# Two decoder-like layers on one core: twelve probability buffers for the second layer's attention, comparisons on another engine, a new order of stages

## The chip, the core and the metric

The kernel runs on one core of a Trainium2 chip. A core has a matrix engine (TensorE, in the profile PE, with its weight loads as PEld), three engines for elementwise work (VectorE as DVE, ScalarE as ACT, GpSimd as POOL) and a sync engine (SP) that here issues nearly all transfers. Each engine takes its instructions in one fixed order; semaphores make one engine wait for another. The metric is the device time in microseconds (us) of one execution. Three executions of the kernel before took 678.07, 679.97 and 681.12 us, median 679.97 us.

## What is computed

The input is a batch of 4 sequences of 512 tokens with 256 channels, in f32. Two layers follow, each a "macaron": half a feed-forward block, attention, half a feed-forward block, with a layer norm ahead of each.

```python
x = x + 0.5 * L0_ffn(layernorm(x)); x = x + L0_attn(layernorm(x)); x = x + 0.5 * L0_ffn(layernorm(x))
x = x + 0.5 * L1_ffn(layernorm(x)); x = x + L1_attn(layernorm(x)); x = x + 0.5 * L1_ffn(layernorm(x))

# L0_ffn: weights are integers minus 128 with a scale per row; silu(gate) * up, then down; hidden 704
# L0_attn: 16 heads of 16 channels, rotary embedding, causal softmax
# L1_ffn: weights made ternary; sigmoid(x @ w1.T) * (x @ w2.T), then @ w3.T
def _quantize(w):
    gamma = jnp.mean(jnp.abs(w))
    return jnp.clip(jnp.round(w / (gamma + EPS)), -1.0, 1.0)
# L1_attn: 16 query heads, 4 key/value heads, ALiBi slopes as bias, causal softmax, output bias
```

## The kernel before, in words

All activations stay in on-chip memory: `X[b]` holds one sequence as 128 partitions x 4 chunks x 256 channels. There are 24 stages of coarse work, for each sequence `b` and layer `L` a feed-forward, an attention and a feed-forward, and they are mixed with each other.

How the order comes about matters here. Every stage is cut into small closures (one tile of a matmul with its evaluation, one score unit, one load). Each closure gets a due time from the table `PLAN` (line 32), in units of one head group of attention; there are 32 such groups, and a unit is a little under 20 us. The closures are sorted by due time (line 694) and recorded in that order. A scheduler of the framework then sets each engine's final order, from that order, the dependencies and the buffers that are free. So an edit of one number in `PLAN`, or of the engine of one operation, may move instructions on all engines.

**Attention.** Each sequence and layer has four groups `g` of four heads. The queries and keys of a group are stacks `Qs[g]` and `Ks[g]` in bf16, 128 partitions x 4 heads x 512 tokens: three bf16 parts of each number, stacked so that one bf16 matmul gives a product of nearly f32 accuracy. `fills(g)` (line 429 and on) loads the stacks from DRAM, with three transfers of 128 KB for `Qs` and, in layer 0, three for `Ks`, issued by SP. In layer 1 there are only 4 key heads in all, so one stack per sequence is enough: `kst` (line 500) takes `Ks[b % 2]`. `Ks[2]` and `Ks[3]` are not used in layer 1, and the rotary tables `cst` (cosine and sine) are not either.

`pass1(g)` (line 503) computes scores in a PSUM tile of tag "s" (four buffers, shared with pass 2), and VectorE takes the row maximum under the mask (line 517, a custom instruction and a short one that reads the accumulator). `fin` (line 521) transposes the maxima and sends them as two more rows into `Qs[g]`, so that pass 2 subtracts the maximum in the matmul itself. `pass2(g)` (line 538) computes the scores transposed (line 557), ScalarE takes the exponential into a buffer of tag "P" (lines 553 and 562), GpSimd sets the part above the diagonal to zero (line 564), and `pv` (line 568) multiplies with the values, for four heads at once on four groups of 32 columns of the matrix engine. The tag "P" has `NP` = 6 buffers of 128 x 512 f32. An exponential into a used buffer waits until the `pv` matmul that read it is done.

**Feed-forward.** `mtile` (line 306) is four matmuls of 128 x 512 into a PSUM tile, with the activations split into a high and a low part. `act` (line 319) is the activation: ScalarE and VectorE read the tile, and GpSimd or VectorE make the low part (line 353). `down` (line 359) is the second projection.

**Layer 1's ternary weights.** `load_ffn1` (line 165) reads the 11 pieces of the three weight matrices twice. The first round (`sums`) takes the sum of absolute values on ScalarE (line 173), 12 instructions with an accumulator; `level` (line 176) makes the thresholds `thr`; the second round (`quant`, line 187) loads each piece again into one of the four buffers of tag "tmp" and makes `(w > t) - (w < -t)` in two instructions: the `is_lt` comparison on GpSimd (line 190), then `is_gt` with the subtraction on VectorE (line 191). Eight pieces have 128 x 352 elements (into `GU[1]`), three 128 x 512 (into `WD[1]`). The feed-forward blocks share the tag "tmp". The rounds are due at `PLAN["w1"]`.

Of the kernel before, what the change touches and what calls it, by code (L numbers as in the profile page):

```python
# [10 lines left out]
F32 = mybir.dt.float32  # L11
# [4 lines left out]
ALU = mybir.AluOpType  # L16
# [4 lines left out]
T = 512  # L21
# [8 lines left out]


PLAN = {
    "lnw": 0.1082, "dw": 0.02, "va": -3.2452, "w1": (3.23, 5.1402, 5.278, 5.8437), "la": 10.0549, "lo": 17.0054,
    "F000": (-4.7797, -3.9955, 0.5991, 0.627), "F010": (-2.4824, -1.3829, 0.446, 0.02),
    "F020": (-1.3638, -1.0988, 0.2537, 0.02), "F030": (0.0651, 4.5821, 0.553, 0.052),
    "F001": (5.6832, 7.2392, 0.5108, 0.5201), "F100": (8.4901, 9.5646, 0.227, -0.008),
    "F011": (10.2798, 11.8688, 0.4612, -0.091), "F110": (12.6033, 13.3522, 0.4119, -0.0508),
    "F021": (13.7131, 15.2214, 0.2194, 0.6814), "F120": (16.1663, 17.4558, 0.1237, 0.057),
    "F031": (17.7427, 19.2089, 0.1794, 0.3572), "F130": (20.6648, 21.4405, 0.097, 0.191),
    "F101": (22.2359, 24.7912, 0.25, 0.0563), "F111": (25.133, 28.5272, 0.2253, 0.559),  # L40
    "F121": (30.9876, 31.9389, 0.3174, 0.35), "F131": (32.8792, 34.4424, 0.45, -0.035),
    "q": (-5.4943, -4.6753, -4.4887, -3.8, -3.9803, -3.4013),
    "q0": (-2.5968, -2.298, -2.236, -1.8988, -1.881, -2.3597),
    "q1": (-0.825, -0.405, -0.485, 0.081, -0.5019, 0.7836), "fill0": -1.2442, "fill": 0.044,
    "p1": (0.0178, 1.0178), "p10": (-1.1381, -0.5831), "p11": (-0.4778, -0.4629), "p2": (-0.0092, 0.9501),
    "post": (4.1583, 4.2211), "f2": 0.0459,
}
# [4 lines left out]
NP, NTMP, NRT, NH, NH5 = 6, 4, 4, 5, 1  # L52
# [4 lines left out]
def macaron(ctx, tc, x, gu0, wd0, s0, sd0, wa0, wq1, wkv1, wo1, bo1, gu1, wd1,  # L57
            cs, krow, qrow, out):
    nc = tc.nc
    V, S, G, PE, SY = nc.vector, nc.scalar, nc.gpsimd, nc.tensor, nc.sync  # L60

    con = ctx.enter_context(tc.tile_pool(name="con", bufs=1))
    wrk = ctx.enter_context(tc.tile_pool(name="wrk", bufs=2))
# [18 lines left out]
    for i in range(2):  # L82
# [12 lines left out]
                    fill=NEG, base=0, channel_multiplier=1)  # L95
# [30 lines left out]
    def load_ffn0():  # L126
# [12 lines left out]
        for k in range(3):  # L139
            w = wrk.tile([128, 2, D], I32, tag="P", name=f"wds{k}", bufs=NP)  # L140
            SY.dma_start(w, wd0[:, 2 * k:2 * k + 2])
# [5 lines left out]
    thr = con.tile([128, 6], F32, name="thr")  # L147
# [17 lines left out]
    def load_ffn1():  # L165

        def sums(n, i, src):
            def f():
                if n == 0:
                    G.memset(ab, 0.0)  # L170
                w = piece(src, f"ws{n}")
                for k, v in enumerate([w] if n < 10 else [w[:, 0], w[0:64, 1]]):
                    S.activation(v, v, AF.Abs, accum_out=ab[0:v.shape[0], n + k:n + k + 1])
            return f

        def level():
            V.tensor_reduce(sm[:, 0:2], ab[:, 0:8].rearrange("p (i n) -> p i n", i=2), AX.X, ALU.add)
            V.tensor_reduce(sm[:, 2:3], ab[:, 8:12], AX.X, ALU.add)
            pg = pmm.tile([128, 512], F32, tag="mm", name="pgam")
            ones = wrk.tile([128, T], F32, tag="tmp", name="ones", bufs=NTMP)[:, 0:128]  # L180
            G.memset(ones, 1.0)
            PE.matmul(pg[:, 0:3], ones, sm[:, 0:3], start=True, stop=True)
            V.tensor_scalar(thr[:, 0:3], pg[:, 0:3], 1.0 / (HID * D), EPS_Q, ALU.mult, ALU.add)
            V.tensor_scalar(thr[:, 3:6], thr[:, 0:3], -0.5, None, ALU.mult)
            V.tensor_scalar(thr[:, 0:3], thr[:, 0:3], 0.5, None, ALU.mult)

        def quant(n, i, src, dst):
            def f():
                w = piece(src, f"wq{n}")
                G.tensor_scalar(dst, w, thr[:, 3 + i:4 + i], None, ALU.is_lt)  # L190
                V.scalar_tensor_tensor(dst, w, thr[:, i:i + 1], dst.bitcast(F32), ALU.is_gt, ALU.subtract)
            return f

        ps = list(ffn1_pieces())
        return ([sums(n, i, s) for n, (i, s, d) in enumerate(ps)] + [level] +
                [quant(n, i, s, d) for n, (i, s, d) in enumerate(ps)])
# [6 lines left out]
    cst = con.tile([128, 2, T], F32, name="cst")  # L203
# [39 lines left out]
    Ks = [con.tile([128, 4, T], BF, name=f"Ks{i}") for i in range(4)]  # L243
# [135 lines left out]
        return th, [act(i) for i in ((0, 1, 2, 5, 3, 4) if first else (5, 0, 1, 2, 3, 4))], [down(0), down(1)]  # L379


    def attn(L, b, tag):
        quick = L == 0 and b == 0
        th, xo = layernorm(b, tag, "xa", 1, halves=quick)
        va = VA[b % 2]
# [114 lines left out]
        def kst(g):  # L500
            return Ks[g] if L == 0 else Ks[b % 2]
# [36 lines left out]
        def pass2(g):  # L538
            Q, K = Qs[g], kst(g)
            nr = mr + 2  # L540
            o = [None]
            def steep(h):

                return L == 1 and g == 0 and h == 0

            pt = {}

            def expo(kc, hs):

                def f():  # L550
                    N = T - 128 * kc
                    n = len(hs)
                    P = wrk.tile([128, T], F32, tag="P", name=f"P{g}{kc}{hs[0]}{tag}", bufs=NP)
                    P = P[:, 0:n * N].rearrange("p (h n) -> p h n", h=n)
                    p = psc.tile([128, T], F32, tag="s", name=f"s2_{g}{kc}{hs[0]}{tag}")
                    for i, h in enumerate(hs):
                        PE.matmul(p[:, i * N:i * N + N], K[0:nr, h, kc * 128:(kc + 1) * 128],  # L557
                                  Q[0:nr, h, kc * 128:T], start=True, stop=not steep(h))
                        if steep(h):
                            PE.matmul(p[:, i * N:i * N + 128], identb, maskT, start=False, stop=True)  # L560
                        pt[kc, h] = P[:, i]
                    pt["last"] = S.activation(P, p[:, 0:n * N].rearrange("p (a n) -> p a n", n=N), AF.Exp, scale=0.25)
                    if not steep(hs[-1]):
                        pt["last"] = G.affine_select(P[:, :, 0:128], P[:, :, 0:128], pattern=[[0, n], [1, 128]],
                                                     compare_op=ALU.is_ge, fill=0.0, base=0, channel_multiplier=-1)
                return f

            def pv(kc):


                def f():
                    if kc == 0:
                        o[0] = pov.tile([128, T], F32, tag="o", name=f"o{g}{tag}")
                    with tc.high_priority(20):
                        for h in range(4):
                            hv = 4 * g + h if L == 0 else h
                            m = PE.matmul(o[0][32 * h:32 * h + 32, kc * 128:T], va[:, kc, hv * VS:hv * VS + 32],  # L577
                                          pt[kc, h], start=kc == 0, stop=kc == 3)
                            if kc < 3 and h < 3:
                                tc.add_manual_dep(m.ins if hasattr(m, "ins") else m, (pt["last"].ins if hasattr(pt["last"], "ins") else pt["last"]).name, AFTER, reason="side by side")  # L580
                return f

            us = []
            for kc in range(NC):
                n = (1, 1, 2, 4)[kc]
                us += [expo(kc, tuple(range(h, h + n))) for h in range(0, 4, n)] + ([pv(kc)] if kc < 2 else [])
            us += [pv(2), pv(3)]

            ot = [None]

            def evac():
                ot[0] = wrk.tile([128, T], F32, tag="oT", name=f"oT{g}{tag}", bufs=1)
                S.copy(ot[0], o[0])

            def fin():
                if g == 0:
                    co["c"] = wrk.tile([128, NC, D], F32, tag="ctx", name=f"ctx{tag}", bufs=1)
                ctxt, oT = co["c"], ot[0]
                pt = pmm.tile([128, NC, 4, 32], F32, tag="mm", name=f"ot{g}{tag}")
                for c in range(NC):  # L600
                    PE.transpose(pt[:, c].rearrange("p i e -> p (i e)"), oT[:, c * 128:(c + 1) * 128], ident)
                ri = wrk.tile([128, NC, 4, 1], F32, tag="ri", name=f"ri{g}{tag}")
                V.reciprocal(ri, pt[:, :, :, 16:17])
                V.tensor_tensor(ctxt[:, :, 64 * g:64 * g + 64].rearrange("p c (i e) -> p c i e", e=16),
                                pt[:, :, :, 0:16], ri.to_broadcast([128, NC, 4, 16]), ALU.mult)

            return us + [evac], fin
# [64 lines left out]
    w1 = load_ffn1()  # L672
# [4 lines left out]
    for n in range(8):  # L677
        a = at[n]
        q = PLAN[f"q{n}"] if f"q{n}" in PLAN else [4 * n + v for v in PLAN["q"]]
# [107 lines left out]
```

## Time and profile before

The profiled execution took 676.93 us; its span, from the first to the last instruction, is 675.2 us, so 1.7 us lie around it. That execution is 3.04 us below the median of the three others.

| Engine | busy us of 675.2 | instructions |
|---|---|---|
| PE (matmul) | 643.1 | 4394 |
| PEld (weight load) | 435.1 | 4394 |
| DVE | 527.5 | 1683 |
| ACT | 450.5 | 872 |
| POOL | 396.5 | 643 |

How to read it: matmuls are pipelined, and the matrix engine's records overlap, so "busy" is not full speed; what helps is the idle time of PE, stage by stage, and what ended it. The other engines' busy time tells where they could not have taken more work. The transfers move 45.46 MB, at a mean of 67 GB/s.

### The profile page before, as it was taken

What the parts mean: (1) busy time and instruction counts of PE and PEld (TensorE: products, weight loads), DVE (VectorE), ACT (ScalarE), POOL (GpSimd) and SP (SyncE); (2) the same over time, 40 slices, a digit from 0 to 9 for tenths busy, and PEclk for the clock granted to TensorE, in tenths of its full rate; (3) what the DMA queues carried; (4) which work ended last, traced back from release to release, by engine and by line L of the source; (5) the groups of instructions that cost most, each with busy time, mean ns of one, the idle gap of its engine ahead of it and who ended that gap; (6) DMA issues with size and microseconds to landing.
All of it is one profiled execution on the core that took longest, in us unless ns stands there. A gap on an engine that the chain in (4) does not pass through costs nothing.

```text
span 675.2 us, 13288 instructions
## 1 busy us (share of the span) xinstructions
PE 643.1 (95%) x4394; PEld 435.1 (64%) x4394; DVE 527.5 (78%) x1683; ACT 450.5 (67%) x872; POOL 396.5 (59%) x643
## 2 busy tenths in 40 slices
PE   7798899998989999999999999999999999999987
PEld 5677566455635776667676757767676675565676
DVE  7788899788799797877868686887879678885354
ACT  3674658785668487685858685785847767648633
POOL 3653958666599765586448755595445544434511
PEclk8998999999999999999999999999999999999999
DMA  8204503244442223112210221001200221100000
GB/s 278 91 0 142 141 1 127 73 129 127 148 138 60 83 73 94 43 34 67 65 29 27 74 60 41 25 24 50 60 26 25 70 83 33 50 3 33 0 33 33
DMA packets 30900, 45.46 MB, mean 67 GB/s; under 512 B 6098, under 2 KB 23754, under 8 KB 30830
## 3 DMA queue, kind: packets, MB, share of 16 engines
q1 hardware_dynamic: 30254, 43.88, 21.4%
q10 hardware_dynamic: 576, 0.72, 0.4%
q8 instruction: 35, 0.57, 0.4%
q14 instruction: 35, 0.29, 0.1%
HBM read 32.00 MB, written 12.32 MB: 66 GB/s over the span
## 4 chain that ended last, share of the span: by engine, by line
PE 72%; DVE 9%; DMA 6%; ACT 5%; POOL 4%; issue 3%; SPq 0%; DVEq 0%; ACTq 0%; POOLq 0%
PE pf L315 18%; PE df L367 10%; PE o0a L577 3%; PE o1a L577 3%; PE o2a L577 3%; PE o3a L577 3%; PE po0a L630 2%; PE po1a L630 2%; PE ltf L293 2%; POOL GU L190 1%; DMA wa0s<-in_wa_dram 1%; DMA ws<-in_gu_dram 1%; PE lta L293 1%; DMA gus<-in_gu_dram 1%; PE pq0a L396 1%
## 5 line engine op out<-in xcount | busy, mean ns | idle before, releaser
L315 PE MATMUL pf<-xhf,GU 128*128 128x512 f32 x352 | 122.7, 436 | 4.7 <-ACT xhf L295 2.2
L353 POOL TENSOR_TENSOR hlf<-hf,hhf 128x512 fp32r<-128x512 f32 x72 | 94.1, 1308 | 45.4 <-ACT hhf L352 45.1
L315 PE MATMUL pf<-xlf,GU 128*128 128x512 f32 x352 | 110.2, 400 | 0.6 <-DVE xlf L296 0.5
L557 PEld LDWEIGHTS <-Ks 98*128 98x128 bf16 (+1 forms) x512 | 44.4, 98 | 57.8 <-issue 45.3
L315 PEld LDWEIGHTS pf<-xhf,GU 128*128 128x128 f32 x352 | 61.4, 192 | 27.2 <-ACT xhf L295 5.5
L315 PEld LDWEIGHTS pf<-xlf,GU 128*128 128x128 f32 x352 | 65.8, 189 | 17.1 <-DVE xlf L296 1.5
L513 PEld LDWEIGHTS <-Qs 96*128 96x128 bf16 (+1 forms) x512 | 43.6, 98 | 45.7 <-issue 33.8
L517 DVE DVE_READ_ACCUMULATOR2_ANT mxt<- 128x1 f32 x512 | 71.2, 139 | 0.2
L352 ACT CAST hhf<-hf 128x512 fp32r<-128x512 f32 x80 | 49.8, 623 | 15.6 <-DVE hf L350 11.2
L350 DVE SCALAR_TENSOR_TENSOR hf<-tf,pf 128x512 f32<-128x512 f32 (+1 forms) x48 | 33.0, 686 | 32.3 <-PE pf L315 15.9
L367 PE MATMUL df<-WD,hhf 128*128 128x256 f32 x320 | 55.5, 291 | 2.6 <-ACT hhf L352 2.6
L367 PE MATMUL df<-WD,hlf 128*128 128x256 f32 x320 | 51.8, 287 | 0.2 <-DVE hlf L353 0.2
L367 PEld LDWEIGHTS df<-WD,hhf 128*128 128x128 f32 x320 | 45.5, 192 | 4.6 <-ACT hhf L352 3.0
L367 PEld LDWEIGHTS df<-WD,hlf 128*128 128x128 f32 x320 | 43.9, 191 | 2.1 <-issue 1.4
L345 POOL TENSOR_TENSOR hf<-tf,hf 128x512 f32<-128x512 f32 x30 | 39.3, 1311 | 9.1 <-ACT hf L344 7.0
L289 ACT ACTIVATE xnf<-X,mrf,rsf 128x256 f32<-128x256 f32 x60 | 31.9, 596 | 14.5 <-POOL mrf L269 9.6
L349 ACT ACTIVATE tf<-pf 128x512 f32<-128x512 f32 (+1 forms) x48 | 28.3, 595 | 19.4 <-PE pf L315 19.2
L295 ACT CAST xhf<-ltf 128x512 fp32r<-128x512 f32 x32 | 18.5, 588 | 20.3 <-PE ltf L293 20.2
L341 ACT ACTIVATE tf<-pf,sgh 128x512 f32<-128x512 f32 (+1 forms) x36 | 25.0, 694 | 6.6 <-PE pf L315 6.1
L372 POOL TENSOR_TENSOR X<-X,dtf 128x512 f32<-128x512 f32 x14 | 18.4, 1316 | 18.1 <-DVE dtf L371 15.9
L342 DVE SCALAR_TENSOR_TENSOR tf<-tf,pf 128x512 f32<-128x512 f32 (+1 forms) x36 | 24.5, 681 | 4.2 <-ACT tf L341 4.1
L261 DVE BATCH_NORM_STATS2 bsf<-X 128x6 f32<-128x256 f32 x64 | 23.5, 413 | 3.6 <-POOL X L372 1.9
(534 smaller groups left out, 2065.1 us busy)
## 6 DMA issues: line engine op xcount, KB each, us to landing
Qs<-drqa SPq DMA_DIRECT2D x96, 128.0 KB
Ks<-drka SPq DMA_DIRECT2D x60, 128.0 KB
out_dram<-X SPq DMA_DIRECT2D x8, 256.0 KB
X<-in_x_dram SPq DMA_DIRECT2D x3, 512.0 KB
drka<-raka SPq DMA_DIRECT2D x4, 384.0 KB
drka<-rcka SPq DMA_DIRECT2D x4, 384.0 KB
drqa<-raqa SPq DMA_DIRECT2D x4, 384.0 KB
drqa<-rcqa SPq DMA_DIRECT2D x4, 384.0 KB
```

The lines of the kernel that those rows point to most:

```text
L289: S.activation(xn[c], X[b][:, c], AF.Identity, bias=mr[:, i:i + 1], scale=rs[:, i:i + 1])
L315: PE.matmul(p, w[:, m:m + 128], xx[:, k], start=n == 0, stop=n == 3)
L345: G.tensor_tensor(h, t, h, ALU.mult)
L349: S.activation(t, g, AF.Tanh, scale=0.5)
L350: V.scalar_tensor_tensor(h, t, 1.0, u, ALU.add, ALU.mult)
L352: S.copy(hh, h)
L353: (V if big and i % 2 or (first or last and big) and i > 2 else G).tensor_tensor(hl, h, hh.bitcast(F32), ALU.subtract)
L367: PE.matmul(p[:, cc], ho[l, i][:, ts], WD[L][:, i], start=n == 0, stop=n == 10)
L513: PE.matmul(p[:, i * st:i * st + N], Q[0:mr, h, c * 128:(c + 1) * 128], K[0:mr, h, 0:N], start=True, stop=True)
L517: V.tensor_tensor_reduce(pi, pi, mask[:, T - N:T], 1.0, FLOOR, ALU.add, ALU.max, mx[:, h, c:c + 1])
L557: PE.matmul(p[:, i * N:i * N + N], K[0:nr, h, kc * 128:(kc + 1) * 128], Q[0:nr, h, kc * 128:T], start=True, stop=not steep(h))
L577: m = PE.matmul(o[0][32 * h:32 * h + 32, kc * 128:T], va[:, kc, hv * VS:hv * VS + 32], pt[kc, h], start=kc == 0, stop=kc == 3)
```

## The change

Three things are changed.

1. In `quant`, the comparison `is_lt` is issued on VectorE instead of GpSimd.
2. In layer 1, every second probability tile takes its room from a rotation of six: two halves of each of `Ks[2]` and `Ks[3]`, seen as f32, and the two halves of `cst`. The others keep the tag "P" with its six buffers.
3. Nine numbers in `PLAN` are changed, among them the beginning of the `sums` round (3.23 to 3.7945) and the due time of the stack loads (`fill`, 0.044 to 0.4489 units after the reference point). The rest shift by up to 0.34 units.

```diff
 PLAN = {
-    ... "w1": (3.23, 5.1402, 5.278, 5.8437) ...
+    ... "w1": (3.7945, 5.1402, 5.278, 5.8437) ...
-    "F020": (-1.3638, -1.0988, 0.2537, 0.02)
+    "F020": (-1.3638, -1.0988, 0.0794, 0.02)
-    "F001": (5.6832, 7.2392, ...)   "F110": (12.6033, 13.3522, ...)   "F130": (20.6648, 21.4405, ...)
+    "F001": (5.6832, 7.3715, ...)   "F110": (12.6033, 13.1578, ...)   "F130": (20.6648, 21.4499, ...)
-    "q": (-5.4943, ...)   "q1": (-0.825, -0.405, -0.485, 0.081, -0.5019, 0.7836)   "fill": 0.044
+    "q": (-5.4589, ...)   "q1": (-0.825, -0.3982, -0.485, 0.081, -0.5019, 1.1219)   "fill": 0.4489
...
         def quant(n, i, src, dst):
             def f():
                 w = piece(src, f"wq{n}")
-                G.tensor_scalar(dst, w, thr[:, 3 + i:4 + i], None, ALU.is_lt)
+                V.tensor_scalar(dst, w, thr[:, 3 + i:4 + i], None, ALU.is_lt)
                 V.scalar_tensor_tensor(dst, w, thr[:, i:i + 1], dst.bitcast(F32), ALU.is_gt, ALU.subtract)
...
+    used = [0]
+
+    def spare():
+
+        used[0] += 1
+        room = [k.rearrange("p h t -> p (h t)").bitcast(F32)[:, T * i:T * i + T] for k in Ks[2:] for i in range(2)]
+        room += [cst[:, i] for i in range(2)]
+        return room[used[0] // 2 % 6] if used[0] % 2 else None
...
-                    P = wrk.tile([128, T], F32, tag="P", name=f"P{g}{kc}{hs[0]}{tag}", bufs=NP)
+                    P = spare() if L == 1 else None
+                    if P is None:
+                        P = wrk.tile([128, T], F32, tag="P", name=f"P{g}{kc}{hs[0]}{tag}", bufs=NP)
```

## The prediction

> **What bounds the kernel now.** First the page: the chain that ended last and the busy shares.
>
> ```profile
> span 675.2 us, 13288 instructions
> PE 643.1 (95%) x4394; PEld 435.1 (64%) x4394; DVE 527.5 (78%) x1683; ACT 450.5 (67%) x872; POOL 396.5 (59%) x643
> PE 72%; DVE 9%; DMA 6%; ACT 5%; POOL 4%; issue 3%; SPq 0%; DVEq 0%; ACTq 0%; POOLq 0%
> ```
>
> PE is the bound, and 32.1 us of the span (675.2 - 643.1) are all that it stands idle. A gain has to come out of these, so I cut them by stage. The columns of the next view are the stretch, its length, busy us (with instructions) of PE, PEld, DVE, ACT and POOL, then clock, DMA share and GB/s.
>
> ```profile
> 134.00:149.00 15.00, 14.78 (x98) 8.28 (x97) 12.59 (x44) 12.16 (x28) 9.51 (x16) 1.00 0.42 126
> 149.00:165.00 16.00, 13.23 (x93) 7.74 (x92) 13.24 (x44) 11.20 (x30) 10.50 (x17) 1.00 0.44 139
> 165.00:179.00 14.00, 14.00 (x120) 11.65 (x113) 9.08 (x31) 6.13 (x13) 7.58 (x13) 1.00 0.49 152
> 179.00:190.00 11.00, 10.46 (x73) 5.80 (x72) 10.80 (x43) 8.98 (x22) 9.14 (x16) 1.00 0.36 100
> 190.00:206.00 16.00, 12.65 (x98) 5.79 (x96) 15.64 (x48) 10.27 (x21) 15.93 (x21) 1.00 0.57 165
> 206.00:222.00 16.00, 15.27 (x90) 9.67 (x91) 13.44 (x47) 13.34 (x25) 15.67 (x23) 1.00 0.19 52
> 343.00:600.00 257.00, 254.82 (x1837) 169.61 (x1836) 203.87 (x698) 180.07 (x347) 144.20 (x249) 1.00 0.14 43
> ```
>
> The reader is to see two things: from 343 to 600, nearly all of layer 1's attention, PE idles 2.2 us of 257; from 179 to 206 it idles 3.9 us of 27, and there both POOL (15.93 of 16 in the second part) and DVE (15.64 of 16) are full. Third, what PE waited for in 179 to 207, and the two lines of the ternary weights with the nearest row for the moved comparison (line 124: one source, one constant, the same shapes):
>
> ```profile
> PE o2a L577 <- POOL P203a L564: 1.2, 1, 1.2
> PE o1a L577 <- POOL P130a L564: 0.8, 1, 0.8
> PE s_021a L513 <- DVE mxt L517: 0.4, 1, 0.4
> ```
>
> ```profile
> L190 POOL TENSOR_SCALAR GU<-wq,thr x8: 1158/1181/1758, 185.1 to 196.8; 128x352 fp32r<-128x352 f32 x8
> L190 POOL TENSOR_SCALAR WD<-wq,thr x3: 1564/1564/1994, 200.3 to 204.4; 128x512 fp32r<-128x512 f32 x3
> L191 DVE SCALAR_TENSOR_TENSOR GU<-wq,thr,GU x8: 570/592/840, 186.7 to 198.6; 128x352 fp32r<-128x352 f32 x8
> L191 DVE SCALAR_TENSOR_TENSOR WD<-wq,thr,WD x3: 743/747/1162, 203.8 to 206.9; 128x512 fp32r<-128x512 f32 x3
> ...
> L124 DVE TENSOR_SCALAR GU<-gus x4: 311/326/340, 5.4 to 9.0; 128x352 fp32r<-128x352 int32 x4
> L124 DVE TENSOR_SCALAR WD<-wds x3: 427/428/555, 11.5 to 13.3; 128x512 fp32r<-128x512 int32 x3
> ```
>
> **Part 1, the comparison leaves POOL.** Line 190 took 10.5 + 5.1 = 15.6 us of POOL in 185 to 206. The triangle selections (line 564) stood between these, and two `pv` groups of PE waited for them: 0.82 at 191.6 and 1.23 at 196.9 in the timeline, together 2.05 us. That is the price of POOL on PE here, and all of it may go. The most that could go is PE's whole idle time of 179 to 206, 3.9 us.
>
> **Part 1, it arrives on DVE.** Eight pieces at the line-124 median of 326 ns and three at 428: 2.61 + 1.28 = 3.9 us. Upper bound: as long as line 191, 8 x 0.592 + 3 x 0.747 = 7.0 us. Lower bound: if POOL's traffic is what stretches line 191 from its shortest (570 and 743) to its means (641 and, from 743, 747 and 1162, 884), then 8 x 0.07 + 3 x 0.14 = 1.0 us comes back and 2.9 remain. I take 3.9, since line 124 is nearest in form. What covers it? DVE's idle time in 179 to 206 is 0.20 + 0.36 = 0.56 us; after 206 it has 16 - 13.44 = 2.56. So at 206 DVE is 3.9 - 0.6 = 3.3 us late. Behind the moved instructions in DVE's queue stand the row maxima of the next groups (line 517): until they have read a score tile, PE can't have one of the four "s" buffers back, and PE's fixed order has score matmuls every microsecond here. In the timeline DVE began row maxima 1.1 to 1.4 us after their matmul (192.6 to 193.7, 197.9 to 199.2): PE runs that much ahead, so of 3.3 us I let the buffers swallow 1.1, and PE is 2.2 us late at 206, the POOL waits gone but swallowed by this. From 206 to 222 DVE can catch up 2.56, but PE only its own idle time there, 0.73: net **+1.5 us**. Bounds: -3.9 (POOL alone paced the stretch) and +6.4 (7.0 - 0.6, nothing recovered).
>
> The Trainium skill speaks on both sides here. *GPSIMD Engine Reference*, section "Performance versus the Vector engine", says that VectorE is about twice as fast for elementwise work; by that the moved pieces would take half of 1181 and 1564 ns, 8 x 0.59 + 3 x 0.78 = 7.1 us, an estimate; line 124 against line 190 shows 3.6 times, and the sum goes by that. *Advanced Engine Details and Errata*, section "VectorE Performance Modes", says that a VectorE instruction in a two-port mode and a GpSimd instruction block each other; by it the moved pieces would hold POOL up for as long as they last, so that POOL would gain 11.7 us (15.6 - 3.9) in place of 15.6. No run here shows that yet; the spread of line 191 (570 to 840) while POOL was full is of that kind.
>
> **Part 1, a new wait in DVE's queue.** The moved instruction also waits for its piece's load. A load can start when line 191 has freed its "tmp" buffer four pieces earlier. In the built program's order, DVE has some 4.8 us of work between that release and the comparison (one comparison 0.33, three of line 191 at 0.52 from start to start, two row maxima of 512 columns at 0.73, two short ones 0.43 and 0.48, one low part 0.60). A load of the same kind took from 154.46 (issue on SP) to 157.16, and the next from 155.57 to 160.15, until ScalarE could use them: 2.7 to 4.6 us, plus 0.5 of issue; and pieces 4 to 6 stand behind stack loads on SP (0.6 us an issue). So pieces 4, 5 and 6 may come 0 to 1 us late each. On POOL such a wait held up the selections alone; on DVE it holds up everything. I take +0.5, bounds 0 and +4 (seven pieces, a little over half a microsecond each).
>
> **Part 2, six more probability buffers.** In layer 1, ScalarE waited ten times for a `pv` matmul ahead of an exponential, 9.7 us in total (line 562 released by o0a, o2a, o3a after 313 us). These waits go. But PE has nothing to gain: of its waits in 343 to 600 one is on a probability tile (POOL P013a, 0.3 us), and PE's order there is the same in both builds but for a handful of instructions. Spread over 257 us, the other 2.2 us of idle time end on DVE. I take **-0.3**; bounds -2.2 (all idle time there) and +0.5 (the new rooms in the key stacks are free only when layer 0's last score matmuls have read them; that order is kept in both builds, two groups apart). No instruction is added.
>
> **Part 3, the order.** Up to 139 us the built orders are equal on every engine, so 20% of the span can't change; the changed part is 139 to 345 us, and PE's work per group moves there by at most 1.9 us from one group to the next. Three of the `sums` instructions (0.50 + 0.19 us) move from 142-145 to 149-155, where ScalarE is full: 3 x 0.6 (their spacing) = 1.8 us late on ScalarE, covered by its wait of 3.16 us for the next weight load at 157.2; if that cover is gone, the context cast (line 618), for which PE waited 1.2 us at 161.6, comes up to 1.8 later. On SP, weight loads 5 to 7 still stand behind GpSimd's query parts (lines 413 and 414), so that wait stays. Stack loads move by a place or two among 311 transfers. `pv` groups that are torn apart on PE, and so run twice (275.1 and 276.7 in the timeline, one more microsecond), are 8 before and 6 after, but by their widths 3.4 us of repeated work in both. I take 0, bounds -2 and +2.
>
> **Sum.** 1.5 + 0.5 - 0.3 + 0 = +1.7 us on a span of 675.2, with the 1.7 around it 678.6 for an execution like the profiled one. The median of the runs is 3.0 above that execution, so 679.97 + 1.7 = **681.7 us**: +0.25%, which counts as no change: 0.5% (3.4 us) is about what a measurement of this kernel can tell from none, since its three runs lie 3 us apart. Range of this case alone 677 to 683.4.
>
> **Rivals.** *POOL was the pace-maker* (faster): both its waits and the PE idle time behind them go, DVE's 3.9 us slide behind 206. For it: PE's longest waits in 179 to 206 are on POOL, one on DVE. Against: DVE had 0.56 us free. 679.97 - 3.9 - 0.7 (idle of 206 to 222) = 675.4. Chance 0.18, with the case in it that the buffers of part 2 count (9.7 us were 670).
>
> *DVE becomes the bound* (slower): the comparisons sit in a full queue and also wait for loads; it decides once a load takes longer than about 4.8 us from release to landing, or the comparison takes over 0.5 us. 3.9 + 4 + 1.8 (context cast) - 2.6 (DVE's idle time after 206) = +7.1, hence 687. Chance 0.32.
>
> *The rooms are not free* (part 2 does not do what it says): exponentials would wait on whole stacks instead of halves. The build shows waits on single tiles, so this has 0.02, within slower.
>
> **Numbers.** Forecast 0.50, faster 0.18, slower 0.32. The range takes in the faster rival's figure and the slower one's: 675 to 687.
>
> **What would show it.** Line 190 as DVE rows of 0.3 to 0.5 us at 185 to 207; POOL under 10 of 16 us in 190 to 206; PE's waits on P130 and P203 gone, with waits on DVE's row maxima in their place, and the group after 206 beginning about 2 us later; the stretch 343 to 600 as long as before within 1 us; the first 139 us alike. I am wrong if PE's idle time in 179 to 222 falls by over 3 us, if comparisons wait for loads by more than 2 us in all, or if layer 1's stretch shortens by more than 2 us.

## The result, and the profile after

The changed kernel took 681.09 us (median of 22 runs, 677.77 to 683.79), the kernel before 679.05 us in 22 runs of the same comparison (676.30 to 682.22). The ratio is 1.0029, with a 95% interval from 1.0016 to 1.0043: 2.0 us slower, inside the half per cent that the prediction called no change, but not nothing. The forecast was 681.7 us.

The page of the changed kernel's profiled execution begins so:

```profile
span 681.1 us, 13261 instructions
PE 647.7 (95%) x4394; PEld 437.4 (64%) x4394; DVE 532.0 (78%) x1694; ACT 450.2 (66%) x872; POOL 382.2 (56%) x632
PE 71%; DVE 11%; DMA 5%; ACT 5%; POOL 4%; issue 3%; SPq 0%; DVEq 0%; ACTq 0%; POOLq 0%
```

Eleven instructions left POOL (14.3 us less) and eleven came to DVE (4.5 us more; 3.3 us against the changed kernel with the comparison back on GpSimd, 528.7 us, so that the rest belongs to the other two parts), and DVE's share of the chain that ended last rose from 9% to 11%. This span is 5.9 us longer than that of before, three times the difference of the medians, so a part of it belongs to the executions and not to the kernels; which part is shown at the end of this section.

By stretch of time (columns as in the prediction: stretch, length, busy us of PE, PEld, DVE, ACT and POOL, then clock, DMA share, GB/s), the changed kernel:

```profile
179.00:190.00 11.00, 10.27 (x80) 5.75 (x79) 8.93 (x38) 7.16 (x19) 5.68 (x14) 1.00 0.48 139
190.00:206.00 16.00, 12.79 (x84) 5.37 (x76) 15.61 (x51) 9.41 (x19) 4.60 (x11) 1.00 0.45 129
206.00:222.00 16.00, 14.66 (x80) 8.29 (x78) 14.26 (x43) 10.55 (x20) 8.45 (x13) 0.89 0.23 66
222.00:247.00 25.00, 25.00 (x179) 17.50 (x178) 21.81 (x66) 14.85 (x28) 20.73 (x27) 1.00 0.20 66
343.00:600.00 257.00, 255.16 (x1829) 170.15 (x1827) 205.73 (x704) 180.23 (x348) 146.46 (x254) 1.00 0.15 45
```

In 190 to 206 us POOL fell from 15.93 to 4.60, and PE gained nothing by it: 12.79 busy against 12.65. DVE was full before (15.64) and is full now (15.61). The windows stand at the same times in both profiles, but the changed kernel is 5 to 6 us late there, so they hold not quite the same work; the stretch that is defined below compares like with like. Behind 222 us PE is full in both, so what is late by then stays late. What PE waited for in 179 to 222 us, changed kernel:

```profile
PE s_110a L522 <- DVE mxt L526: 0.8, 1, 0.8
PE pf L315 <- DVE mts3a L537: 0.6, 1, 0.6
PE s_323a L522 <- DVE mxt L526: 0.5, 1, 0.5
PE s_020a L522 <- ACT P203a L573: 0.5, 1, 0.5
PE s_213a L568 <- ACT P212a L573: 0.5, 1, 0.5
...
PE s_100a L522 <- DVE mxt L526: 0.3, 1, 0.3
...
PE o2a L588 <- POOL P203a L575: 0.2, 1, 0.2
```

Of the two waits on GpSimd's selections (2.05 us together) 0.2 is left. In their place stand waits on DVE, 2.4 us against 0.4 in the kernel before, 1.8 of them on row maxima, and waits on ACT's exponentials and casts, 2.3 us against 1.1. ACT itself waited once, 1.5 us, for line 191 (0.3 us before). Last, the ternary weights, each line by itself (min, median and max in ns, then first and last start):

```profile
L190 DVE TENSOR_SCALAR GU<-wq,thr x8: 381/396/402, 189.3 to 200.0; 128x352 fp32r<-128x352 f32 x8
L190 DVE TENSOR_SCALAR WD<-wq,thr x3: 481/483/628, 206.3 to 210.8; 128x512 fp32r<-128x512 f32 x3
its engine sat idle before it (us, times) until:
  DMA wq<-in_gu_dram: 0.3, 1
```

```profile
L191 DVE SCALAR_TENSOR_TENSOR GU<-wq,thr,GU x8: 566/578/768, 191.4 to 202.5; 128x352 fp32r<-128x352 f32 x8
L191 DVE SCALAR_TENSOR_TENSOR WD<-wq,thr,WD x3: 659/747/1650, 208.9 to 213.3; 128x512 fp32r<-128x512 f32 x3
```

The records of the comparison add up to 8 x 0.396 + 3 x 0.53 = 4.8 us; it waited once for a load, 0.3 us. Records on DVE overlap a little, so that its busy time rises by less (3.3 us, above).

**What belongs to the executions.** The most exact reading of two profiles is the start of one and the same matmul in both: here the first score matmul of an attention group (line 513 or 522). Its lateness against the profile of before, in us, by where it stands there:

| Start in before | 71.6 | 149.1 | 169.3 | 187.8 | 202.3 | 245.5 | 342.0 | 397.1 | 601.5 |
|---|---|---|---|---|---|---|---|---|---|
| changed kernel | +1.82 | +1.82 | +3.51 | +4.86 | +5.77 | +6.89 | +7.99 | +7.18 | +6.47 |
| comparison on VectorE alone | +0.45 | +0.52 | +1.55 | +2.73 | +4.72 | +4.76 | +4.89 | +4.88 | +4.89 |
| rooms alone | +1.27 | +1.27 | +2.99 | +2.99 | +2.97 | +2.35 | +2.35 | +1.73 | +1.01 |

The first column spreads over 3.5 us among the fourteen profiles of this case though the orders are equal there; kernels with the new PLAN lie from -0.37 to +3.13, the others from 0 to +1.83. Then the rooms-alone kernel, whose built order equals that of before over more than half of TensorE's queue, loses 1.72 us between 149 and 169 us. The reason is the granted clock. Changed kernel, and below it the kernel before:

```profile
166.00:168.00 2.00, 2.00 (x13) 0.85 (x12) 2.00 (x6) 2.00 (x5) 1.24 (x3) 0.50 0.01 4
...
210.00:212.00 2.00, 1.68 (x6) 1.09 (x6) 2.00 (x7) 1.58 (x4) 0.29 (x1) 0.56 0.65 195
```

```profile
60.00:62.00 2.00, 2.00 (x11) 2.00 (x11) 1.54 (x3) 1.57 (x3) 0.60 (x1) 0.50 0.17 41
...
166.00:168.00 2.00, 2.00 (x20) 2.00 (x19) 1.81 (x5) 1.02 (x2) 2.00 (x3) 1.00 0.27 72
```

The last four columns are POOL, clock, DMA share and GB/s. Twice here PE has half its clock for 3.4 us, 1.7 us lost each time; behind 40 us the profile of before has such a dip at 59 us only. So the readings below take one stretch, from the fourth group of sequence 1 in layer 0 (169.3 us in before) to the first group of layer 1 (342.0), 172.7 us in before, and subtract what the clock took inside it.

### The profile page after: what moved, and what is told of

Same layout as the page of the kernel before. It is cut to its first block, busy times and chain, and to the rows that moved or that the text cites. A ratio compares the mean times of both kernels' runs of the same rounds, so it can differ in the third digit from the quotient of the medians.

```text
span 681.1 us, 13261 instructions
## 1 busy us (share of the span) xinstructions
PE 647.7 (95%) x4394; PEld 437.4 (64%) x4394; DVE 532.0 (78%) x1694; ACT 450.2 (66%) x872; POOL 382.2 (56%) x632
## 4 chain that ended last, share of the span: by engine, by line
PE 71%; DVE 11%; DMA 5%; ACT 5%; POOL 4%; issue 3%; SPq 0%; DVEq 0%; ACTq 0%; POOLq 0%
PE pf L315 19%; PE df L367 11%; PE o3a L588 3%; PE o1a L588 3%; PE o0a L588 3%; PE o2a L588 2%; PE po1a L641 2%; PE po0a L641 2%; DMA wa0s<-in_wa_dram 1%; PE ltf L293 1%; PE lta L293 1%; PE pq0a L405 1%; PE pq1a L405 1%; DMA gus<-in_gu_dram 1%; DVE mxt L526 1%
## 5 line engine op out<-in xcount | busy, mean ns | idle before, releaser
L367 PEld LDWEIGHTS df<-WD,hlf 128*128 128x128 f32 x320 | 45.3, 197 | 1.2 <-issue 1.0
L575 POOL TENSOR_SCALAR_AFFINE_SELECT Ks<-Ks 128x128 f32<-128x128 f32 (+2 forms) x54 | 18.8, 349 | 34.7 <-ACT Ks L573 34.2
```

Source lines behind the costliest of these rows:

```text
L367: PE.matmul(p[:, cc], ho[l, i][:, ts], WD[L][:, i], start=n == 0, stop=n == 10)
```

## The experiments

The three parts can be had one by one, and all eight combinations were run. "Stretch" is the difference to before of the 172.7 us just named, clock dips subtracted, from one profile each. The experiments ran in three groups, each with its own runs of before, medians 678.03 us (rows 1 to 4), 679.06 (rows 5, 6, 8 and 9) and 678.91 (rows 10 to 13); the changed kernel's row is the comparison above. The ratio is estimated from the single runs and is not the quotient of two medians: for rooms alone that quotient is 0.9980, for GpSimd with the round to 7.7 units 0.9990, both inside their intervals.

| Kernel | median us | ratio to before, 95% interval | stretch us |
|---|---|---|---|
| comparison on VectorE alone | 682.22 | 1.0063 [1.0038, 1.0087] | +3.3 |
| rooms alone | 676.68 | 0.9969 [0.9951, 0.9986] | -0.6 |
| new PLAN alone | 680.09 | 1.0024 [1.0003, 1.0044] | +0.3 |
| changed, comparison back on GpSimd | 678.20 | 0.9994 [0.9974, 1.0014] | -0.1 |
| changed, without the rooms | 681.85 | 1.0039 [1.0025, 1.0054] | +2.7 |
| changed, with the old PLAN | 680.09 | 1.0023 [1.0005, 1.0042] | +3.1 |
| changed | 681.09 | 1.0029 [1.0016, 1.0043] | +2.8 |
| changed, weights' round ends at 7.9 units | 686.87 | 1.0111 [1.0089, 1.0133] | +4.6 |
| changed, each comparison twice | 687.58 | 1.0132 [1.0106, 1.0158] | +6.8 |
| changed, weights' round ends at 7.4 | 680.17 | 1.0016 [1.0000, 1.0032] | +1.6 |
| rooms, GpSimd, round ends at 7.7 | 678.24 | 0.9983 [0.9967, 0.9999] | -0.1 |
| rooms, VectorE, round ends at 7.7 | 683.51 | 1.0062 [1.0043, 1.0081] | +3.6 |
| rooms, three comparisons on VectorE | 677.87 | 0.9983 [0.9968, 0.9998] | +0.6 |

**Each part alone, and part 1 undone.** The first four kernels, in the order of the table. The letters of the theories hold within one group of runs. Comparison on VectorE alone:

```diff
-                G.tensor_scalar(dst, w, thr[:, 3 + i:4 + i], None, ALU.is_lt)
+                V.tensor_scalar(dst, w, thr[:, 3 + i:4 + i], None, ALU.is_lt)
```

> The kernel before with the is_lt comparison on VectorE alone, old table, no extra rooms. Theory A (the forecast: VectorE is full from 179 to 206 us, so the moved work lands on PE): 2.0 us slower (1.5 for the work, 0.5 for waits on loads), ratio 1.003. Theory B (GpSimd paced that stretch): 2 to 4 us faster, ratio 0.995 to 0.997, and the new table costs what the whole change costs. Theory C (the parts are all free, the difference is in the buffers): 1.000.

Rooms alone (the kernel before with `spare()` and its use):

```diff
-                    P = wrk.tile([128, T], F32, tag="P", name=f"P{g}{kc}{hs[0]}{tag}", bufs=NP)
+                    P = spare() if L == 1 else None
+                    if P is None:
+                        P = wrk.tile([128, T], F32, tag="P", name=f"P{g}{kc}{hs[0]}{tag}", bufs=NP)
```

> The kernel before with the six extra probability rooms alone. Theory A: 0.3 us faster, ratio 0.9995 (between 0.997 and 1.001); ScalarE's ten waits on probability products after 313 us (9.7 us) gone, PE's idle time from 343 to 600 us as before within 1 us. Theory B: the same. Theory C: 2 us slower or more, 1.003.

The new PLAN alone (the table's hunk of the change, nothing else):

> The kernel before with the new table alone. Theory A: no change, ratio 1.000 (between 0.997 and 1.003). Theory B: slower by more than the whole change, 1.005 or more, since the comparison's move then gains. Theory C: 1.000.

The changed kernel with the comparison back on GpSimd (the first diff, reversed):

> The changed kernel with the is_lt comparison back on GpSimd; new table and extra rooms stay. Theory A: 2.0 us faster than the changed kernel, so level with the kernel before, 1.000. Theory B: slower than the changed kernel, 1.006 or more of the kernel before. Theory C: as the changed kernel, 1.003.

Measured: +0.63%, -0.31%, +0.24% and, undone, 0.9994. The comparison on VectorE costs time with nothing else changed, and its lateness arises where the prediction put it: in the table of lateness it goes from +1.55 to +4.72 us between 169 and 202 us and is never made good. The rooms are worth much more than was forecast. The result of 2 us is a difference of larger parts.

**The other combinations.** The changed kernel without the rooms, then with the old PLAN:

```diff
-                    P = spare() if L == 1 else None
+                    P = None
```

> The changed kernel without the six rooms (comparison on VectorE and the new PLAN stay). Theory A, the three parts add up, each at its own place: part 1 and the PLAN measured alone gave +0.63% and +0.24%, so 1.0087 of the kernel before; from the changed kernel's side, 1.0029 + 0.0031 = 1.006. So 1.006 to 1.009 (683 to 685 us), and in 380 to 397 us and after 575 us the group marks are 0.5 us each later again than in the changed kernel. Theory B, the rooms pay only in the old order of stages: within 0.001 of the changed kernel, 1.002 to 1.004.

```diff
-    "lnw": 0.1082, "dw": 0.02, "va": -3.2452, "w1": (3.7945, 5.1402, 5.278, 5.8437), "la": 10.0549,
+    "lnw": 0.1082, "dw": 0.02, "va": -3.2452, "w1": (3.23, 5.1402, 5.278, 5.8437), "la": 10.0549, "lo": 17.0054,
...
```

> The changed kernel with the old PLAN (comparison on VectorE and the rooms stay). Theory A, the parts add up: 0.63 - 0.31 = +0.32%, or 0.29 - 0.24 = +0.05%; 1.0005 to 1.003 (678.5 to 680.2 us), not slower than the changed kernel. Theory B, the new PLAN was chosen for the other two parts and takes some of part 1's cost away: slower than the changed kernel, 1.004 to 1.007. Beside this, the marks of the first 72 us (all orders equal there) tell whether the later start of 1.8 to 3.1 us that four profiles with the new PLAN showed belongs to the PLAN (then it is gone here, 0 to 1.3 us) or to the executions.

With all eight, each part's price is the mean of four differences. Part 1: 0.63, 0.54, 0.15 and 0.35, mean 0.42% or 2.8 us. Rooms: -0.31, -0.40, -0.30 and -0.10, mean -0.28% or -1.9 us. PLAN: 0.24, 0.25, -0.24 and 0.06, mean 0.08% or 0.5 us. Taking the single intervals (half-widths of 0.13 to 0.25) as independent, such a mean is good to about 0.15%, 1 us. So part 1's loss and the rooms' gain are shown, and PLAN's effect is not told from nothing. PLAN looks dearer beside GpSimd comparisons (0.24, 0.25) than beside VectorE ones (-0.24, 0.06), so that the second theory has something for it; these numbers do not settle it. The late starts of the first 72 us are not PLAN's: without the rooms but with the new PLAN the first group begins at -0.37 us, with the old PLAN at +1.06.

**Is it VectorE's time, or the new order?** Any of these edits also reorders TensorE's queue. So VectorE's work was doubled with the same operation:

```diff
                 V.tensor_scalar(dst, w, thr[:, 3 + i:4 + i], None, ALU.is_lt)
+                V.tensor_scalar(dst, w, thr[:, 3 + i:4 + i], None, ALU.is_lt)
```

> The changed kernel with each comparison of the ternary weights issued twice on VectorE, 11 more instructions of 0.40 to 0.53 us, 4.8 us. Theory A, VectorE has no time left in 185 to 210 us, and what it recovers after 206 is used up: 3 to 4.8 us slower than the changed kernel, 1.007 to 1.010. Theory C, VectorE's time is mostly hidden behind the score buffers and the loss came from the order: under 1 us, 1.003 to 1.0045.

And the weights' second round was spread, so that the comparisons leave the full stretch:

```diff
-    "w1": (3.7945, 5.1402, 5.278, 5.8437)
+    "w1": (3.7945, 5.1402, 5.278, 7.9)
```

> The changed kernel with the second round of the ternary weights spread over 2.62 units in place of 0.57 (its end 5.8437 to 7.9; the weights are needed at 8.5). Theory A, part 1 costs because the comparisons sit in a stretch where VectorE is full: with some 45 us in place of 20, VectorE's idle time (1.7 of 16 us in 206 to 222, more after) takes the 4.8 us, and the kernel is 1.5 to 2.5 us faster than the changed one: 0.999 to 1.0005. Theory C, the loss comes from the order that the scheduler makes on TensorE's queue and not from VectorE's load: no gain, 1.002 to 1.005.

Both were slower than either theory had it, 1.03% and 0.82% above the changed kernel. The lateness of the groups tells why: both lose 3.6 us behind 397 us (from there to the last group 207.3 us each, against 203.7 in the changed kernel and 203.7 or 203.8 in every other kernel with the rooms). There, far from the edit, their built orders differ from the changed kernel's up to 87% of TensorE's queue. PE's waits from 397 to 601 us, for the kernel spread to 7.9 units:

```profile
PE pf L315 <- DVE hf L350: 1.0, 2, 0.7
PE s_200a L522 <- DVE mxt L526: 0.4, 1, 0.4
PE ot3a L612 <- ACT oT3a L604: 0.3, 1, 0.3
PE pf L315 <- DVE mts0a L537: 0.3, 1, 0.3
```

and for the one spread to 7.4 units, whose order behind 42% is that of the changed kernel:

```profile
PE s_022a L568 <- DVE mxt L526: 0.5, 1, 0.5
PE pf L315 <- DVE hf L350: 0.4, 1, 0.4
PE o0a L588 <- POOL P013a L575: 0.2, 1, 0.2
```

So an edit at 190 us turned the order of the second layer into another one, and 3.6 us of each loss are that: PE is idle there some 2.4 us longer and busy some 1.2 us longer. What remains is the stretch, for the doubling 6.8 against 2.8, 4.0 us more for eleven more comparisons. Doubled kernel, stretch by stretch and the second comparison's line:

```profile
190.00:206.00 16.00, 12.58 (x78) 5.36 (x78) 16.00 (x56) 9.26 (x18) 6.06 (x12) 1.00 0.34 96
206.00:222.00 16.00, 12.88 (x75) 6.47 (x75) 15.87 (x49) 9.59 (x18) 7.50 (x11) 1.00 0.36 98
```

```profile
L191 DVE TENSOR_SCALAR GU<-wq,thr x8: 383/396/568, 190.8 to 202.9; 128x352 fp32r<-128x352 f32 x8
L191 DVE TENSOR_SCALAR WD<-wq,thr x3: 484/486/942, 212.4 to 217.8; 128x512 fp32r<-128x512 f32 x3
```

DVE is now full over 32 us and PE idles 6.5 of them. Some 5 us more of VectorE's records cost 4.0 us. But doubling changes the order too: in the traces TensorE's instructions stand in another order than the changed kernel's from 25% of its queue on, inside the stretch. So this run agrees with the theory of VectorE's time and doesn't separate it from the order. Least reordered are the two pairs on the new PLAN that differ in the comparison alone: 103 of PE's 4394 places, all between 24% and 27% of its queue. Their stretches differ by 2.9 us (with the rooms) and 2.4 us (without).

What the stretch is made of tells more. Kernel before, comparison on VectorE alone, comparison back on GpSimd and changed kernel, each from the same matmul to the same matmul (the last has one clock dip inside, 1.7 us):

```profile
169.33:342.01 172.68, 167.97 (x1163) 111.80 (x1161) 140.67 (x466) 120.42 (x236) 122.90 (x188) 1.00 0.27 80
170.89:346.90 176.01, 169.83 (x1162) 111.35 (x1161) 144.27 (x477) 120.48 (x236) 108.43 (x177) 1.00 0.25 79
173.71:346.28 172.57, 167.41 (x1166) 111.06 (x1165) 142.00 (x464) 121.10 (x238) 123.06 (x189) 1.00 0.26 80
172.84:350.00 177.16, 170.61 (x1166) 112.17 (x1165) 145.47 (x475) 121.84 (x238) 109.03 (x178) 0.99 0.26 78
```

DVE is busy 3.6 and 3.5 us longer, and the stretch is 3.3 and 2.9 us longer. Only 1.5 and 1.4 us of that are idle time of PE; the rest, 1.9 and 1.5 us without the dip, is longer busy time of PE for the same matmuls. In the other two unspread pairs (with the rooms on the old PLAN; without them on the new) DVE is busy 3.7 and 2.7 us longer, PE's idle time grows by 2.1 and 0.7, its busy time by 1.7 in both. With the new PLAN 1.0 us of it are `pv` matmuls (28.28 us of records in place of 27.24). So a third to a little over half of part 1's price is PE standing idle; where the rest came from is shown for those `pv` matmuls alone, and no run takes the loaded engine and the new order apart.

**Spreading, without the far change of order.** 7.4 and 7.7 units were taken because the built order then differs from its neighbour's only ahead of 42%:

```diff
-    "w1": (3.7945, 5.1402, 5.278, 5.8437)
+    "w1": (3.7945, 5.1402, 5.278, 7.4)
```

> The changed kernel with the second round of the ternary weights ending at 7.4 units in place of 5.8437 (7.9 had been tried: 1.0111, of which 3.5 us lay behind 397 us, where its built order differed from the changed kernel's up to 87% of TensorE's queue; at 7.4 the built order differs from the changed kernel's only between 26% and 42%). Theory A, full VectorE is what part 1 costs: 1.5 to 2.5 us faster than the changed kernel, 0.9995 to 1.001, and the marks behind 397 us follow the changed kernel's. Theory C, the density is not it: 1.002 to 1.005, and part 1's cost is the same wherever the comparisons are put.

On the old PLAN with the rooms, comparisons on GpSimd and on VectorE:

```diff
-    "w1": (3.23, 5.1402, 5.278, 5.8437)
+    "w1": (3.23, 5.1402, 5.278, 7.7)
```

> The kernel before with the six rooms and the second round of the ternary weights ending at 7.7 units; comparisons on GpSimd, old PLAN otherwise. To be read against rooms alone (0.9969). Theory A: in 185 to 235 us neither GpSimd nor VectorE is full any more, PE's waits there fall: 0.994 to 0.997. Theory C: 0.997 to 1.000.

> As the run before, but with the comparisons on VectorE: part 1 where the stretch is not full. To be read against it and against the same without the spread (1.0023). Theory A: part 1's cost falls from 0.54% there to 0.2% or less, so 0.995 to 0.999. Theory C, part 1 costs the 4.8 us of VectorE wherever it stands: 0.5 to 0.7% above the run before, 1.000 to 1.004.

Against the same kernel unspread, spreading cost 0.14% with GpSimd and 0.39% with VectorE, and gave 0.13% in the changed kernel; the first and the last can't be told from nothing. Part 1's price in the spread pair is 0.79%, not lower than the 0.54% of the dense pair: the theory that the full stretch makes the price, and that room lies behind it, found no support; with VectorE the kernel came out slower than either theory had it (1.0062). The windows of the kernel spread to 7.7 with VectorE, and its waits of PE in 179 to 250 us:

```profile
206.00:222.00 16.00, 12.97 (x80) 7.43 (x78) 16.00 (x46) 11.05 (x21) 12.87 (x17) 1.00 0.32 98
222.00:247.00 25.00, 22.32 (x149) 16.06 (x147) 22.87 (x62) 9.86 (x19) 16.72 (x23) 0.86 0.27 86
```

```profile
PE mt1a L534 <- DVE mxt L526: 2.1, 1, 2.1
PE s_121a L522 <- DVE mxt L526: 1.2, 1, 1.2
```

Spreading moves line 191 as well, so more than the 4.8 us goes into a part where DVE had 2.56 of 16 us free. DVE is full to the last tenth in 206 to 222, and PE waits for row maxima there instead, one of them 2.1 us (0.86 in the second window is another clock dip). The two lines also took longer, as their rows and one moment of the timeline show:

```profile
L190 DVE TENSOR_SCALAR GU<-wq,thr x8: 388/692/1421, 186.3 to 218.8; 128x352 fp32r<-128x352 f32 x8
L191 DVE SCALAR_TENSOR_TENSOR GU<-wq,thr,GU x8: 569/1014/1356, 188.2 to 220.1; 128x352 fp32r<-128x352 f32 x8
...
203.34 1.29 POOL L353 TENSOR_TENSOR hlf<-hf,hhf 128x512 fp32r<-128x512 f32 x1 [1.05 <-ACT hhf L352]
...
203.40 1.42 DVE L190 TENSOR_SCALAR GU<-wq,thr 128x352 fp32r<-128x352 f32 x1
```

The comparison began just after a GpSimd instruction of 1.29 us had begun; it took 1.42 us and ended 0.2 us after it. Over all fourteen profiles the comparisons on VectorE with no GpSimd instruction beside them took 380 to 406 ns (128 x 352, 30 of them) and 474 to 490 ns (128 x 512, 11); the nine that took 0.9 to 1.4 us all ran beside a TENSOR_TENSOR of GpSimd, and all are in spread or doubled kernels. Together the records of lines 190 and 191 on VectorE are 18.6 us here, against 13.1 us in the same kernel unspread; with GpSimd, spreading took line 191 from 7.7 to 10.2 us. So the spread kernels didn't carry the same work into free room, they had more of it, and they don't refute the theory either. Which placement would be cheapest was not settled: the stretch lost 1.6, 3.6 and 4.6 us at three ends of the round.

**A part of part 1.** Only the three 128 x 512 comparisons on VectorE:

```diff
-                G.tensor_scalar(dst, w, thr[:, 3 + i:4 + i], None, ALU.is_lt)
+                (V if i == 2 else G).tensor_scalar(dst, w, thr[:, 3 + i:4 + i], None, ALU.is_lt)
```

> The kernel before with the six rooms, and only the three comparisons of the 128 x 512 pieces on VectorE, which stand at 203 to 207 us, ahead of the stretch in which VectorE has time; the eight others stay on GpSimd. The built order moves 74 instructions of TensorE's queue only. Theory A: three of the eleven instructions, 1.5 of 4.8 us, and 2.5 us of idle time just behind: 0 to +0.1% on rooms alone, 0.997 to 0.998. Theory C, the cost goes with the number of comparisons moved: +0.15%, 0.9985. Rival B, GpSimd's backlog after 206 us counts: faster than rooms alone, 0.994 to 0.996.

0.9983, 0.14% above rooms alone, though the interval doesn't exclude the same time; the stretch is 1.2 us above it. That is nearest to the theory by which the cost goes with the number (3/11 of part 1's 2.8 us is 0.8), and against a gain from GpSimd's relief. None of the mixed versions beat rooms alone, which has the lowest ratio of all, 0.9969, and is faster than both kernels; its interval overlaps those of the two at 0.9983.

## Why the prediction was right, and where it was not

The time was right to 0.6 us, and so was the direction of the first two parts, but the terms of the sum were wrong with opposite signs and cancelled: measured less forecast, +0.8 us for the comparison, -1.6 for the rooms, +0.5 for PLAN. That the sum is so near, +1.7 against 2.0 measured, is luck. The start differed too, 679.97 us from three runs against 679.05 from 22.

1. *GpSimd's price on PE (2.05 us, "all of it may go"): held.* The waits went (0.2 left), POOL has 4.60 busy of 16.
2. *The comparisons' time on VectorE (3.9 us): too small by the records, about right by the busy time.* The records are 396 and some 530 ns, 4.8 us in all. Line 124 has a constant, and an int32 source, where line 190 reads its threshold from memory, one per partition; that form was taken as alike. DVE's busy time in the stretch rose by 2.7 to 3.7 us in the four pairs, since records overlap. The hoped-for return by a faster line 191 did not come: its eight short pieces got 0.3 us shorter, its three long ones 0.4 us longer, 7.8 us before and 7.9 after.
3. *"Of 3.3 us I let the buffers swallow 1.1 ... catch up ... only its own idle time there, 0.73: net +1.5": the direction held, the two reliefs did not come.* The kernel with this part alone is 3.2 us later at 202 us than at 169, and 3.3 at 342. This is the term of the sum that was mis-sized: part 1 was forecast at 1.5 + 0.5 = 2.0 us and measured at 2.8 (runs, good to 1 us) and 2.4 to 3.8 (the stretch, five pairs with all eleven comparisons moved and unspread or spread alike). The path was right in part: the forecast has all of it as PE's waiting, and in the four unspread pairs 0.7 to 2.1 us are idle time, 1.5 to 1.9 us longer busy time of PE.
4. *The new wait for loads (+0.5, bounds 0 and +4): 0.3 us, once.* The rival that needed loads to be late fell with this; its other condition, a comparison of over 0.5 us, was met by the three large pieces alone, in the mean.
5. *Rooms (-0.3): mis-sized, -1.9 us, good to 1 us, near the bound of -2.2.* The step that failed: "PE has nothing to gain", since hardly any of its waits was on a probability tile. ScalarE's waits for `pv` ahead of an exponential did fall, from 9.7 us in ten to 5.4 in three. The kernel with the rooms alone, waits of ScalarE from 313 us on:

```profile
ACT P012a L573 <- PE o0a L588: 3.9, 1, 3.9
...
ACT P330a L573 <- PE o3a L588: 0.8, 1, 0.8
...
ACT P303a L573 <- PE o2a L588: 0.7, 1, 0.7
```

   PE's gain lies where the built order shifted by a few score matmuls: in its profile it makes up 0.6 us near 396 us, 0.6 between 577 and 589 (three stalls of 0.28 to 0.38 us gone, one of 0.30 come), and 0.5 behind 601. A probability buffer that comes earlier lets the exponential read its score tile earlier, and PE's next score matmul wants that tile; the prediction counted only waits on the probabilities themselves. That this is the way from the rooms to those stalls is argued, not shown by a run.
6. *PLAN (0, bounds -2 and +2): +0.5, good to 1 us.* Held.

Of the signs that were named: the group that stands at 202.3 us in before began 2.3 us later, counted from the group at 169.3 (from +3.51 to +5.77; "about 2" was said). PE's idle time in 179 to 222 rose from 4.6 to 5.3 us. The stretch 343 to 600 was to be as long as before within 1 us; by the groups from 342.0 to 601.5 it was 1.5 us shorter, the rooms' work, so that this sign failed, though under the 2 us named as a refutation. The rival in which GpSimd set the pace is refuted by the kernel with part 1 alone. The slower rival (687) had the right engine; doubling the work reached its time (687.58), but with 3.6 us that lie behind 397 us.

The prediction cited two places of the Trainium skill. By *Advanced Engine Details and Errata*, section "VectorE Performance Modes", a VectorE instruction in a two-port mode and one on GpSimd block each other. The changed kernel's timeline has a case of that kind (start us, duration us, instruction):

```profile
196.16 0.29 POOL L575 TENSOR_SCALAR_AFFINE_SELECT P202a<-P202a 128x128 f32<-128x128 f32 x1 [1.48 <-ACT P202a L573]
...
200.00 0.38 DVE L190 TENSOR_SCALAR GU<-wq,thr 128x352 fp32r<-128x352 f32 x1
...
200.20 0.84 POOL L575 TENSOR_SCALAR_AFFINE_SELECT P210a<-P210a 128x128 f32<-128x128 f32 x1 [2.09 <-ACT P210a L573]
...
200.31 0.57 DVE L191 SCALAR_TENSOR_TENSOR GU<-wq,thr,GU 128x352 fp32r<-128x352 f32 x1
```

Of two selections of one shape, the one that began inside a comparison, with line 191 right behind it, took 0.84 us, not 0.29, and ended 0.2 us after line 191. That agrees with the rule in kind, as do the nine long comparisons beside GpSimd's work above. In which mode VectorE ran no trace shows, and no run tried the rule by itself. With POOL at 4.60 of 16 us it costs little here; in the spread kernels lines 190 and 191 together were 2 to 6 us longer on VectorE. The Trainium skill's *GPSIMD Engine Reference*, section "Performance versus the Vector engine", says about twice as fast for VectorE, by a measured addition of two inputs; this move showed 1181 to 396 ns, three times. By the page's factor the comparisons would have taken 7.1 us, by the rows they took 4.8.

## What to carry to other kernels

When an engine stands full beside the one that sets the pace, work given to it can cost as much as that engine is busy longer, whatever it relieves: here 2.4 to 3.8 us for 2.7 to 3.7 us. Look whether PE has idle time behind the stretch to catch up in, not whether the loaded engine has, and look at PE's busy time as well as at its waits. Work that is moved can also get longer by its new neighbours: compare the rows of the same line before counting on free room. Buffers can help an engine that hardly waits for them; the likely way, not shown here, is that what fills them holds another buffer that this engine wants. And where a scheduler makes the order, compare the built orders to the end of the program before reading a time: here an edit at 190 us changed the order at 400 to 590 us and cost 3.6 us that had nothing to do with its purpose.

## What the runs showed of the hardware

Between 40 and 660 us the granted clock of PE fell to half for 3.4 us at 56 to 66 us in eleven of the fourteen profiles and at 162 to 172 us in twelve; three profiles have one more at 210 to 242, and two dips were twice as long (162 to 172 and 234 to 242 us). Each 3.4 us cost 1.7 us, nearly as much as the whole change.

The traces show what goes ahead of it. Changed kernel, the 3.41 us ahead of a dip and the dip; below it the kernel before at the same place, without one:

```profile
162.46:165.88 3.42, 2.12 (x12) 1.43 (x13) 2.62 (x8) 3.42 (x10) 0.83 (x3) 1.00 0.00 1
165.88:169.29 3.41, 3.41 (x20) 1.64 (x18) 2.21 (x6) 2.19 (x5) 2.56 (x5) 0.50 0.01 2
```

```profile
157.62:161.03 3.41, 2.47 (x19) 0.99 (x17) 1.73 (x5) 1.77 (x7) 2.84 (x4) 1.00 0.46 141
161.03:164.45 3.42, 2.71 (x16) 1.91 (x16) 3.21 (x9) 3.42 (x9) 1.01 (x4) 1.00 0.00 0
```

In every profile the clock changed only at whole steps of 3.41 us. Cut into these steps, the fourteen profiles have some 2540 between 40 and 660 us. All 26 dips began behind a step in which PE was busy for 63% or less (2.12 of 3.42 us here). All ten steps at 47% or less were followed by a dip, of the 29 between 49% and 63% sixteen were, and behind none of the 2500 above did one begin. So idle time of PE that falls together within one step can cost a second time. The steps don't begin at the same place in every execution: in the kernel before the idle time at 158 to 164 us is spread over two steps, 72% and 79% busy, and no dip follows. Whether one order brings more dips than another was not tried over many executions; the medians hold the dips, and single profiles differ by them.
